# The seam between layer 0 and layer 2 of a four-layer graph kernel: layer 2's first slots over other rows, two tiles' lists gathered there, a weight split moved

## The chip, the cores and the metric

The kernel runs on one core of a Trainium2 chip. A core has engines that work in parallel, each in its own order: PE (TensorE, matrix products), DVE (VectorE) and ACT (ScalarE) for elementwise work, POOL (GpSimd), which here issues indirect transfers, and SP (SyncE), which issues the plain transfers. Sixteen DMA engines move the data between main memory and the on-chip buffers. The metric is the device time of one execution, in microseconds (us); lower is better. A time is the median of several runs.

## The reference

There are 2708 nodes with 512 features (fp32) and one matrix adj (2708 x 2708, nonnegative, mostly zero, denser towards low indices, its diagonal always set). Each of four layers normalizes x per row, applies a ReLU, computes something of it, and adds that to x:

```python
def layer(x, f):  return x + f(relu(layernorm(x)))
# layer 0
mask = (adj > 0); head = mask / sqrt(row_sum(mask))
inc = adj + head; f0 = (inc @ h) / row_sum(inc)
# layer 1: attention with 8 heads, scores - 1e16 * (1 - max(adj, eye)), softmax, values, Wo
# layer 2
h = relu(adj @ (h @ W1) + b1); h = relu(adj @ (h @ W3) + b3); f2 = tanh(h @ Wf + bf)
# layer 3
A = (adj != 0); f3 = A @ (h @ W + b) / column_sum(A)[:, None]
```

The mask of layer 1 is so large that each row's attention falls on the one column where max(adj, eye) is largest. Layer 1 is therefore a gather: with y = h (Wv Wo), row i adds y[argmax of row i].

## The kernel before, in words

Nodes are cut into 22 row tiles of 128 (the last has 20). A tile m's row of adj is used as a few dense 128x128 blocks (WHOLE[m], six at most) and as lists of 128 rows that hold a nonzero (CHUNKS[m], none for tile 0, 10 for tile 1, 9 for tile 2, then fewer). A list's rows of adj, transposed, and of the operand are fetched with indirect transfers on POOL. Tiles 0 to 2 (LEAD) use dense blocks for everything in layer 0, so their lists serve only layer 2 and later.

**Layer 0 and layer 1's y.** The loop over m forms a sum on PE (L866), the new x1 on DVE (L879), its normalization (L194 to L204), its transposes (L210), its product with Wv Wo (`yacc`, L176), the copy `yo` on ACT (L810) and the store of y on SP (L812). `after(m, ...)` holds the last four and runs one to two tiles behind. The stores wait in a list, `pending`, which `flush` issues at the next turn. The operands h of the sums are 128x512 rows (`h0`, `h6`, ...), which the gathers of `gather_rows` (L654) later reuse.

Each tile's whole row of adj (a slab `ar`, 1354 KB) must be scanned: `count_signs` on ACT with a Sign and a Relu pass, `attended` on DVE with a maximum with the identity (L622), MAX8 (L623) and FIND_INDEX8 (L624), which gives the column of the row's maximum. The tiles that are first in the program, 3 to 5 (FIRST) and 0 to 2 (ZERO), have their slabs loaded early for other ends and are scanned late: `LATE = FIRST + ZERO` are loaded again from turn m = 14 on, one a turn (`load_slab`), and scanned one turn later. After the loop, L914 copies the columns found to `idx`. `degrees` loads 18 pieces of counts (L386, SP), sums them on PE (L359) and ends in DVE operations (L368 to L380).

At m = 18 `gather_adj` gathers the lists of tiles 1 and 2 (19 indirect transfers, L635, POOL) and stores them to main memory (`listed`, L645, POOL). At m = 14 a weight W1 is loaded into `wr`, at m = 16 it is split into three parts hi, lo, s (`split_w`, `wa`; four ACT, eight DVE and four ACT operations, `split_b`, L215 to L225), and W3 is loaded into the same `wr`. Two operations named `behind` tie these to that turn.

**Layer 2.** For t = 0 to 21, `fetch(t)` loads x1 of the tile into a slot (L1170, SP) and gathers y by `idx` into another (L1172, POOL). Nine tiles are fetched ahead (AHEAD). Pool `g`, to which the slots belong, is the first one opened after layer 0; it lies where layer 0's slabs were. `first_product(t)` adds the two (L1184, DVE), stores x2 (L1185, SP), normalizes into the y slot, fetches tile t + 9, makes three parts of the ReLU of its transpose (`relu_parts`: transposes L983 on PE, `v_hi` L989 on ACT, `v_lo` and `v_s` on DVE), multiplies with W1's parts (`project3`, L1010, PE: `main` and `mixed`, or `agg` and `aggs` for odd t), drains the two into `go` (L968 on ACT, L969 on DVE) and stores it to `g1d` (L1193). `first_parts(t)` splits `go` into `ghi`, `glo`, `gs` for the dense products. `aggregated(m, ...)` forms adj's row tile times g1: raw blocks of adj (`raw`, L1029, SP) are marked as zero or not (`nz`, L1067, ACT), split (`a_hi` L1093, `a_lo` L1094) and multiplied (L1106); lists are loaded from `listed` (`load_listed`), marked too (`nz<-ac`, L1067) and multiplied with rows of g1 gathered from `g1d` (L1047, POOL). The gathers of g1 rows start when all 22 products are stored. Each finished tile is multiplied with W3 (`g2_rows`). W3 is split (`wb`) right after the nine fetches, and the biases b1, b3 (`load_bias`, L1156) are loaded before them.

The kernel is written in a layer that schedules: the order of instructions on each engine comes from a scheduler that takes the program's order and its own estimates. `tc.issue_after(instr)` makes what is inside follow `instr` in the order. [...]

Of the kernel before, what the change touches and what calls it, by code (L numbers as in the profile page):

```python
# [22 lines left out]
P = 128  # L23
# [21 lines left out]
def kernel(  # L45
# [41 lines left out]
    NCA = max(CHUNKS)  # L87
    NCL = max(CHUNKS[LEAD:])
# [66 lines left out]
    idx_g = const.tile([P, NT - 1, NCH], U32, name="idx_g")  # L155
# [79 lines left out]

    short = ctx.enter_context(ExitStack())
# [7 lines left out]
    with tc.tile_pool(name="l0_slab", bufs=2) as slabs, tc.tile_pool(  # L244
# [16 lines left out]
        idx_a = hp.tile([P, NT, NCH], U32, name="idx_a")  # L261
# [186 lines left out]
        def search(m):  # L448
# [9 lines left out]
            for c0 in range(0, CHUNKS[m], 8):  # L458
                c = slice(c0, c0 + 8)
                at = wp.tile([P, 8], U32, name="found")  # L460
                nc.vector.max_index(at, want[:, c], ranks)
                nc.vector.tensor_scalar(
                    index_g(m)[:, c],
                    at,
# [6 lines left out]
                    idx_a[:, m, c],  # L471
# [10 lines left out]
        def load_h0(ts):  # L482
            for t in ts:
                h0[t] = hp.tile([P, D], FP, name=f"h{t}")
                nc.sync.dma_start(out=h0[t][: rows(t)], in_=x[span(t)])
# [69 lines left out]
        LATE = FIRST + ZERO  # L555
# [72 lines left out]
        def gather_adj(m):  # L628

            n, num = rows(m), CHUNKS[m]  # L630
            for c0 in range(0, num, NCL):
                k = min(NCL, num - c0)
                ac = slabs.tile([P, NCL, P], FP, name="ac", bufs=3)
                for c in range(k):
                    nc.gpsimd.indirect_dma_start(  # L635
                        out=ac[:, c, :n],
                        out_offset=None,
                        in_=adj_units,
                        element_offset=dense_of(m) * P * N + m * P,
                        in_offset=bass.IndirectOffsetOnAxis(  # L640
                            ap=idx_a[:, m, c0 + c : c0 + c + 1], axis=0
                        ),
                    )
                if m < LEAD:
                    nc.gpsimd.dma_start(out=listed[m][:, c0 : c0 + k], in_=ac[:, :k, :n])  # L645
            gathers[m] = ac[:, :k, :n]

        def gather_rows(m):

            gs = []  # L650
            for c in range(CHUNKS[m]):
                g = hp.tile([P, D], FP, name=f"h{DENSE + gather_slot[0] % NGG}")
# [146 lines left out]
        def after(m, hn):  # L799
# [10 lines left out]
            nc.scalar.copy(yo[:n], yacc[:n])  # L810
# [18 lines left out]
        def flush():  # L829
            flush_counts()  # L830
            for issue in pending:
                issue()
            pending.clear()
# [20 lines left out]
        for m in range(NT):  # L854
# [48 lines left out]
            if m == NT - LEAD - 1:  # L903
                for t in range(1, LEAD):
                    gather_adj(t)
            if m == NT // 2 + 3:
                wr = load_w(wset, w1_d, "wr", lambda w: behind(w[:1, 0, :1], xt[:1, :1]))
            if m == NT // 2 + 5:
                w1 = split_w(
                    wset, wr, "wa", lambda w: behind(w[:1, :1], xt[:1, :1])  # L910
                )
                wr = load_w(wset, w3_d, "wr")
# [15 lines left out]

    gp = short.enter_context(tc.tile_pool(name="g", bufs=1))
# [96 lines left out]
    def load_piece(m, ts):  # L1026
        n, k = rows(m), rows(ts[0])
        raw = ap.tile([P, PIECE, P], FP, name="raw", bufs=3)
        nc.sync.dma_start(  # L1029
            out=raw[:k, : len(ts), :n],  # L1030
            in_=adj_t[ts[0] * P : ts[0] * P + k * len(ts), m * P : m * P + n].rearrange(
                "(t p) m -> p t m", p=k
            ),
        )
        return raw[:k, : len(ts), :n], k

    def load_listed(m):
        both = ap.tile([P, NCA + 1, P], FP, name="ac")
        ac = both[:, : CHUNKS[m], : rows(m)]
        nc.sync.dma_start(out=ac, in_=listed[m])  # L1040
# [16 lines left out]
    def aggregate(m, parts, shifted, gd, marked, bias):  # L1057
# [12 lines left out]
        chunks = []  # L1070
        if num:
            ac, spare = load_listed(m)
            if alone(m):
                nc.sync.dma_start(out=spare, in_=gd[span(m)])
                nc.vector.scalar_tensor_tensor(  # L1075
                    spare, spare, diag_c[:, m : m + 1], bias, op0=ALU.mult, op1=ALU.add
# [55 lines left out]
    def aggregated(m, parts, shifted, gd, bias, marked=False):  # L1132
        n = rows(m)
        u = wp.tile([P, D], FP, name="u")
        main, mixed, bias = aggregate(m, parts, shifted, gd, marked, bias)
# [817 lines left out]
```

## Time and profile before

| | us |
|---|---|
| median of 3 runs (1353.71 to 1357.23) | 1355.77 |
| the profiled execution, its own time | 1431.05 |
| span of the profiled execution, core 0 | 1429.2 |
| busy in that span: PE, DVE, ACT, POOL | 1218.8, 924.7, 693.2, 673.6 |
| last sum of layer 0 done | 488.0 |
| last store of y issued | 511.42 |
| first gather of y rows for layer 2 | 514.58 |
| first gather of g1 rows | 636.98 |

The last four rows are positions in the span of the profiled execution. In a timeline line of the profile, the first number is the start, the second the busy time, then engine, source line, operation and tiles; square brackets hold the idle time before it and what ended that. In a line of groups, the numbers after the bar are the total busy time, the mean of one in ns, and the idle time ahead. SPq is SP's queue of issues, PEld the loading of weights on PE.

### The profile page before, as it was taken

How to read it: one execution, taken by the hardware profiler on the slowest of the kernel's cores; microseconds unless marked ns; L12 is line 12 of the kernel's file. 1: busy time of each engine (PE TensorE's matmuls, PEld its weight loads, DVE VectorE, ACT ScalarE, POOL GpSimd, SP SyncE). 2: the span in 40 equal slices, each digit the busy share in tenths (PEclk: the TensorE clock that was granted, in tenths of full speed). 3: DMA queues.
4: the chain of work that ended last, by engine and by line, in shares of the span. 5: the costliest groups of instructions: out<-in, count | busy, mean ns of one | idle time of the engine just before them, and what ended most of it. 6: DMA issues, size and time to landing. Idle time of an engine off the chain costs nothing. (4 is left out here: it accounts for less than half of the span.)

```text
span 1429.2 us, 15148 instructions
## 1 busy us (share of the span) xinstructions
PE 1218.8 (85%) x4223; PEld 726.3 (51%) x4223; DVE 924.7 (65%) x1859; ACT 693.2 (49%) x1098; POOL 673.6 (47%) x703
## 2 busy tenths in 40 slices
PE   4985977769896848999989999899999999958797
PEld 2332433324343326765655655466666666646575
DVE  4664977768899857952343446356667685746576
ACT  5873563648635636642232224245555554634353
POOL 2245457555667441116645543245445344167663
PEclk9977998789988969999999999999999999979898
DMA  9976898778979477638888887856566666488785
GB/s 342 350 251 225 283 302 277 246 249 293 322 253 335 168 254 266 220 128 272 259 261 255 274 248 239 273 177 219 194 212 193 198 190 207 137 313 249 248 250 163
DMA packets 179342, 349.92 MB, mean 245 GB/s; under 512 B 22795, under 2 KB 85525, under 8 KB 175517
## 3 DMA queue, kind: packets, MB, share of 16 engines
q1 hardware_dynamic: 131648, 201.72, 41.5%
q0 software_dynamic: 46032, 145.05, 32.6%
q10 hardware_dynamic: 1568, 2.10, 0.4%
q8 instruction: 35, 0.57, 0.2%
q14 instruction: 59, 0.48, 0.1%
HBM read 285.97 MB, written 62.82 MB: 244 GB/s over the span
## 5 line engine op out<-in xcount | busy, mean ns | idle before, releaser
L1047 POOL DMA_INDIRECT gg<-g2d,idx_g x130 | 141.2, 1086 | 197.1 <-PE aggs L1110 149.3
L1110 PE MATMUL aggs<-gg,ac 128*128 128x512 f32 (+1 forms) x520 | 231.3, 593 | 3.2 <-DMA gg<-g1d,idx_g 2.1
L1047 POOL DMA_INDIRECT gg<-g1d,idx_g x130 | 130.7, 1005 | 159.1 <-PE aggs L1110 86.5
L635 POOL DMA_INDIRECT ac<-in_adj_t_dram,idx_a x130 | 132.7, 1021 | 91.9 <-issue 37.3
L866 PE MATMUL acc<-h,inc 128*128 128x512 f32 (+1 forms) x276 | 143.0, 664 | 37.4 <-DVE inc L706 29.2
L1110 PEld LDWEIGHTS aggs<-gg,ac 128*128 128x128 f32 (+1 forms) x520 | 97.0, 188 | 113.6 <-issue 102.2
L654 POOL DMA_INDIRECT h<-h0d,idx_g x111 | 114.8, 1034 | 83.7 <-PE acc L866 40.8
L866 PE MATMUL acc<-h,incl 128*128 128x512 f32 (+1 forms) x222 | 106.0, 620 | 0.8 <-issue 0.8
L866 PEld LDWEIGHTS acc<-h,inc 128*128 128x128 f32 (+1 forms) x276 | 54.9, 212 | 101.0 <-issue 60.2
L1075 DVE SCALAR_TENSOR_TENSOR ac<-ac,diag_c,bias 128x512 f32<-128x512 f32 x30 | 22.6, 754 | 100.8 <-DMA ac<-g1d 59.1
L1047 POOL DMA_INDIRECT gg<-hidr,idx_g x62 | 70.7, 1140 | 34.6 <-issue 20.8
L176 PE MATMUL yacc<-wvo,hT 128*128 128x512 f32 (+1 forms) x176 | 83.9, 615 | 1.7 <-ACT hT L211 1.0
L1106 PE MATMUL agg<-ghi,a_hi 128*128 128x512 f32 x180 | 77.3, 429 | 0.0
L1106 PE MATMUL agg<-glo,a_lo 128*128 128x512 f32 x180 | 73.4, 408 | 4.2 <-ACT glo L225 4.2
L1106 PE MATMUL aggs<-gs,a_s 128*128 128x512 f32 x180 | 73.1, 406 | 1.3 <-DVE gs L222 1.3
L990 DVE SCALAR_TENSOR_TENSOR v_lo<-pt,v_hi 128x512 fp32r<-128x512 f32 (+1 forms) x88 | 57.0, 658 | 16.2 <-ACT v_hi L989 13.9
L866 PEld LDWEIGHTS acc<-h,incl 128*128 128x128 f32 (+1 forms) x222 | 41.8, 195 | 50.0 <-issue 47.1
L623 DVE MAX8 tops<-ar 128x8 f32<-128x2708 f32 (+1 forms) x22 | 65.4, 2971 | 0.0
L624 DVE FIND_INDEX8 at_top<-tops,ar 128x8 uint32<-128x2708 f32 (+1 forms) x22 | 65.3, 2969 | 0.0
L989 ACT ACTIVATE v_hi<-pt 128x512 fp32r<-128x512 f32 (+1 forms) x88 | 48.2, 575 | 29.0 <-PE pt L983 22.1
L1139 DVE SCALAR_TENSOR_TENSOR u<-aggs,u 128x512 f32<-128x512 f32 x42 | 28.9, 687 | 50.9 <-PE aggs L1110 37.7
L1010 PE MATMUL main<-wb,v_hi 128*128 128x512 f32 (+1 forms) x176 | 56.7, 444 | 5.2 <-ACT v_hi L989 3.4
(355 smaller groups left out, 2777.9 us busy)
## 6 DMA issues: line engine op xcount, KB each, us to landing
ar<-in_adj_dram SPq DMA_DIRECT2D x27, 1354.0 KB
raw<-in_adj_t_dram SPq DMA_DIRECT2D x92, 192.0 KB
slot<-x SPq DMA_DIRECT2D x41, 256.0 KB
at<-in_adj_t_dram SPq DMA_DIRECT2D x26, 256.0 KB
h<-in_x_dram SPq DMA_DIRECT2D x21, 256.0 KB
h0d<-h POOLq DMA_DIRECT2D x21, 256.0 KB
xt<-in_x_dram SPq DMA_DIRECT2D x21, 256.0 KB
x<-xt SPq DMA_DIRECT2D x21, 256.0 KB
```

Of the source, the lines that this page charges most:

```text
L176: nc.tensor.matmul(acc[:n], hT[:, c, :n], w[:, c, :], start=(c == 0), stop=(c == NCD - 1))
L623: nc.vector.max(tops[:n, m, :], ar[:n])
L624: nc.vector.max_index(at_top[:n, m, :], tops[:n, m, :], ar[:n])
L635: nc.gpsimd.indirect_dma_start(out=ac[:, c, :n], out_offset=None, in_=adj_units, element_offset=dense_of(m) * P * N + m * P, in_offset=bas ...
L654: nc.gpsimd.indirect_dma_start(out=g, out_offset=None, in_=h0d[:, :], in_offset=bass.IndirectOffsetOnAxis(ap=index_g(m)[:, c : c + 1], axi ...
L866: product = nc.tensor.matmul(acc[:n], a, g, start=(i == 0), stop=(i == len(pairs) - 1))
L989: nc.scalar.activation(hi[d], pt[d], AF.Relu, scale=UP)
L990: nc.vector.scalar_tensor_tensor(lo[d], pt[d], 0.0, hi[d].bitcast(FP), op0=ALU.max, op1=ALU.subtract)
L1010: nc.tensor.matmul(acc[:n], a[:, c, :n], b[:, c, :], start=first and c == 0, stop=last and c == NCD - 1,)
L1047: nc.gpsimd.indirect_dma_start(out=gs[c], out_offset=None, in_=gd[:, :], in_offset=bass.IndirectOffsetOnAxis(ap=index_g(m)[:, c : c + 1], ...
L1106: turn(nc.tensor.matmul(acc[:n], a[:k, i, :n], b[:k], start=st, stop=sp))
L1110: nc.tensor.matmul(mixed[:n], a, g, start=(c == 0 and not dense_of(m)), stop=(c == len(chunks) - 1),)
```

## The change

1. Layer 0's h rows get a pool of their own (`l0_rows`), opened first, and layer 2's slots get one (`slots`), also opened first; so the slots lie where the h rows were.
2. `LATE` drops tile 0: tile 0 is scanned completely at the start, where its slab is loaded first, and one reload and one late scan go.
3. The lists of tiles 1 and 2 are gathered in layer 2, in `load_listed`, behind the ninth fetch, straight into the tile that is multiplied; two SP stores then write them to `listed`. Their indices are kept in `idx_lead`. In POOL's order these 19 gathers stand between fetches: nine fetches, three lists, fetch 9, seven lists, fetches 10 and 11, nine lists, fetch 12 and on.
4. W1 is split behind the last `yo`, and W3's load follows the last store of y. W3's split stands in `first_product(9)`; its first four ACT operations come out among the norms of the first products.
5. The biases b1 and b3 load behind the store of x2 of tile 2, the raw blocks behind the stores of x2 of tiles 0 and 1, the bias of layer 3 behind the last store of y.
6. `idx_g` is narrower (12 columns), `idx_a` holds tiles 3 and on only.

In the order of ACT's instructions, the marks `nz<-ac` of tiles 1 and 2 move: the first stands right behind the fourth tile's norm, the second twelve instructions further on, behind the fifth; before, they stood behind the sixth and the seventh.

The line numbers of the changed kernel are up to 24 higher from there on. The core of the diff:

```diff
...
@@ -152,7 +154,8 @@
-    idx_g = const.tile([P, NT - 1, NCH], U32, name="idx_g")
+    idx_g = const.tile([P, NT - 1, NCI], U32, name="idx_g")
+    idx_lead = const.tile([P, LEAD - 1, NCH], U32, name="idx_lead")
@@ -233,6 +236,7 @@
+    last_store, last_yo = [None], [None]
     short = ctx.enter_context(ExitStack())
@@ -241,7 +245,9 @@
-    with tc.tile_pool(name="l0_slab", bufs=2) as slabs, tc.tile_pool(
+    with tc.tile_pool(name="l0_rows", bufs=1) as hrows, tc.tile_pool(
+        name="l0_slab", bufs=2
+    ) as slabs, tc.tile_pool(
         name="l0_h", bufs=1
@@ -258,7 +264,7 @@
-        idx_a = hp.tile([P, NT, NCH], U32, name="idx_a")
+        idx_a = hp.tile([P, NT - LEAD, NCH], U32, name="idx_a")
@@ -459,16 +465,17 @@
                 nc.vector.max_index(at, want[:, c], ranks)
+                k = min(8, NCI - c0)
                 nc.vector.tensor_scalar(
-                    index_g(m)[:, c],
-                    at,
+                    index_g(m)[:, c0 : c0 + k],
+                    at[:, :k],
                     float(N - first),
...
                 nc.vector.tensor_scalar(
-                    idx_a[:, m, c],
+                    idx_a[:, m - LEAD, c] if m >= LEAD else idx_lead[:, m - 1, c],
                     at,
@@ -481,7 +488,7 @@
             for t in ts:
-                h0[t] = hp.tile([P, D], FP, name=f"h{t}")
+                h0[t] = hrows.tile([P, D], FP, name=f"h{t}")
                 nc.sync.dma_start(out=h0[t][: rows(t)], in_=x[span(t)])
@@ -552,7 +559,7 @@
         ZERO = list(range(LEAD))
-        LATE = FIRST + ZERO
+        LATE = FIRST + ZERO[1:]
         masks, row, slab = {}, {}, {}
@@ -628,28 +635,24 @@
             n, num = rows(m), CHUNKS[m]
-            for c0 in range(0, num, NCL):
-                k = min(NCL, num - c0)
-                ac = slabs.tile([P, NCL, P], FP, name="ac", bufs=3)
-                for c in range(k):
-                    nc.gpsimd.indirect_dma_start(
-                        out=ac[:, c, :n],
-                        out_offset=None,
-                        in_=adj_units,
-                        element_offset=dense_of(m) * P * N + m * P,
-                        in_offset=bass.IndirectOffsetOnAxis(
-                            ap=idx_a[:, m, c0 + c : c0 + c + 1], axis=0
-                        ),
-                    )
-                if m < LEAD:
-                    nc.gpsimd.dma_start(out=listed[m][:, c0 : c0 + k], in_=ac[:, :k, :n])
-            gathers[m] = ac[:, :k, :n]
+            ac = slabs.tile([P, NCL, P], FP, name="ac", bufs=3)
+            for c in range(num):
+                nc.gpsimd.indirect_dma_start(
+                    out=ac[:, c, :n],
+                    out_offset=None,
+                    in_=adj_units,
+                    element_offset=dense_of(m) * P * N + m * P,
+                    in_offset=bass.IndirectOffsetOnAxis(
+                        ap=idx_a[:, m - LEAD, c : c + 1], axis=0
+                    ),
+                )
+            gathers[m] = ac[:, :num, :n]
...
             for c in range(CHUNKS[m]):
-                g = hp.tile([P, D], FP, name=f"h{DENSE + gather_slot[0] % NGG}")
+                g = hrows.tile([P, D], FP, name=f"h{DENSE + gather_slot[0] % NGG}")
                 gather_slot[0] += 1
@@ -807,7 +810,7 @@
             yo = wp.tile([P, D], FP, name="yo")
-            nc.scalar.copy(yo[:n], yacc[:n])
+            last_yo[0] = nc.scalar.copy(yo[:n], yacc[:n]).ins
             pending.append(
@@ -829,7 +832,7 @@
             for issue in pending:
-                issue()
+                last_store[0] = issue().ins
             pending.clear()
@@ -900,16 +903,8 @@
                 score_bound(xt[:1, :1])
-            if m == NT - LEAD - 1:
-                for t in range(1, LEAD):
-                    gather_adj(t)
             if m == NT // 2 + 3:
                 wr = load_w(wset, w1_d, "wr", lambda w: behind(w[:1, 0, :1], xt[:1, :1]))
-            if m == NT // 2 + 5:
-                w1 = split_w(
-                    wset, wr, "wa", lambda w: behind(w[:1, :1], xt[:1, :1])
-                )
-                wr = load_w(wset, w3_d, "wr")
         flush()
@@ -926,6 +921,7 @@
+    slots = short.enter_context(tc.tile_pool(name="slots", bufs=1))
     gp = short.enter_context(tc.tile_pool(name="g", bufs=1))
@@ -1026,18 +1022,33 @@
         raw = ap.tile([P, PIECE, P], FP, name="raw", bufs=3)
-        nc.sync.dma_start(
-            out=raw[:k, : len(ts), :n],
-            in_=adj_t[ts[0] * P : ts[0] * P + k * len(ts), m * P : m * P + n].rearrange(
-                "(t p) m -> p t m", p=k
-            ),
-        )
+        with tc.issue_after(stored_x[0]):
+            nc.sync.dma_start(
+                out=raw[:k, : len(ts), :n],
+                in_=adj_t[ts[0] * P : ts[0] * P + k * len(ts), m * P : m * P + n].rearrange(
+                    "(t p) m -> p t m", p=k
+                ),
+            )
         return raw[:k, : len(ts), :n], k
-    def load_listed(m):
+    def load_listed(m, marked):
         both = ap.tile([P, NCA + 1, P], FP, name="ac")
         ac = both[:, : CHUNKS[m], : rows(m)]
-        nc.sync.dma_start(out=ac, in_=listed[m])
+        if marked and m < LEAD:
+            with tc.issue_after(last_fetch[0]):
+                for c in range(CHUNKS[m]):
+                    nc.gpsimd.indirect_dma_start(
+                        out=ac[:, c, :],
+                        out_offset=None,
+                        in_=adj_units,
+                        element_offset=dense_of(m) * P * N + m * P,
+                        in_offset=bass.IndirectOffsetOnAxis(
+                            ap=idx_lead[:, m - 1, c : c + 1], axis=0
+                        ),
+                    )
+            nc.sync.dma_start(out=listed[m], in_=ac)
+        else:
+            nc.sync.dma_start(out=ac, in_=listed[m])
         return ac, both[:, -NCD:, :].rearrange("p c k -> p (c k)")
@@ -1054,7 +1065,7 @@
-    def aggregate(m, parts, shifted, gd, marked, bias):
+    def aggregate(m, parts, shifted, gd, marked):
@@ -1067,13 +1078,13 @@
         mixed = ps_a.tile([P, D], FP, name="aggs")
-        chunks = []
+        chunks, bias = [], None
         if num:
-            ac, spare = load_listed(m)
+            ac, spare = load_listed(m, marked)
             if alone(m):
...
                 nc.vector.scalar_tensor_tensor(
-                    spare, spare, diag_c[:, m : m + 1], bias, op0=ALU.mult, op1=ALU.add
+                    spare, spare, diag_c[:, m : m + 1], biases[0 if marked else 1], op0=ALU.mult, op1=ALU.add
                 )
...
@@ -1156,36 +1168,47 @@
-    bias1 = load_bias(b1_d, "bias0")
-    bias3 = load_bias(b3_d, "bias1")
+    last_fetch, stored_x, biases = [None], [None], []
     xs, ys, g1, g1p = {}, {}, {}, {}
...
         n = rows(t)
-        xs[t] = gp.tile([P, D], FP, name=f"slot{t % AHEAD}")
+        xs[t] = slots.tile([P, D], FP, name=f"slot{t % AHEAD}")
         nc.sync.dma_start(out=xs[t][:n], in_=x1[t][:n])
-        ys[t] = gp.tile([P, D], FP, name=f"slot{AHEAD + t % AHEAD}")
-        nc.gpsimd.indirect_dma_start(
+        ys[t] = slots.tile([P, D], FP, name=f"slot{AHEAD + t % AHEAD}")
+        fetched = nc.gpsimd.indirect_dma_start(
             out=ys[t][:n],
...
         )
+        if t + 1 == AHEAD:
+            last_fetch[0] = fetched.ins
...
             return g1[t]
+        nonlocal wr
         n = rows(t)
...
         nc.vector.tensor_add(xt[:n], xt[:n], hn[:n])
-        nc.sync.dma_start(out=x2[t][:n], in_=xt[:n])
+        kept_x = nc.sync.dma_start(out=x2[t][:n], in_=xt[:n]).ins
+        if t < 2:
+            stored_x[0] = kept_x
+        if t == 2:
+            with tc.issue_after(kept_x):
+                biases.append(load_bias(b1_d, "bias0"))
+                biases.append(load_bias(b3_d, "bias1"))
         norm(wp, xt, n, hn)
...
             fetch(t + AHEAD)
+        if t == AHEAD:
+            w3.extend(split_w(wsetb, wr, "wb"))
+            wr = load_w(wset, wf_d, "wr")
         banks = (ps_a, ("agg", "aggs")) if t % 2 else ()
@@ -1203,8 +1226,11 @@
         fetch(t)
-    w3 = split_w(wsetb, wr, "wb")
-    wr = load_w(wset, wf_d, "wr")
+    with tc.issue_after(last_store[0]):
+        with tc.issue_after(last_yo[0]):
+            w1 = split_w(wset, wr, "wa")
+        wr = load_w(wset, w3_d, "wr")
+    w3 = []
@@ -1221,7 +1247,7 @@
             near = relu_parts(sums.pop(last), rows(last))
-        sums[m] = aggregated(m, first_parts, first_product, g1d, bias1, marked=True)
+        sums[m] = aggregated(m, first_parts, first_product, g1d, marked=True)
         if m == 0:
...
```

More of the change, by code (lines that the diff above doesn't have):

```diff
@@ L87 @@
     NCA = max(CHUNKS)
+    NCI = NCH - 4
+    assert all(num <= NCI for num in CHUNKS)
     NCL = max(CHUNKS[LEAD:])
@@ L1130, in aggregate, with aggregated @@
         return main, mixed, bias
-    def aggregated(m, parts, shifted, gd, bias, marked=False):
+    def aggregated(m, parts, shifted, gd, marked=False):
         n = rows(m)
         u = wp.tile([P, D], FP, name="u")
-        main, mixed, bias = aggregate(m, parts, shifted, gd, marked, bias)
+        main, mixed, bias = aggregate(m, parts, shifted, gd, marked)
+        bias = biases[0 if marked else 1] if bias is None else bias
         if dense_of(m):
@@ L1232 @@
     bf = load_bias(bf_d, "bias0")
-    bl = load_bias(b_d, "bias2")
+    with tc.issue_after(last_store[0]):
+        bl = load_bias(b_d, "bias2")
     g2, g2p, x3 = {}, {}, {}
@@ L1239, in second_product @@
             n = rows(t)
-            g2[t] = gp.tile([P, D], FP, name=f"slot{t % NSLOT}")
+            g2[t] = slots.tile([P, D], FP, name=f"slot{t % NSLOT}")
             nc.sync.dma_start(out=g2[t][:n], in_=g2d[span(t)])
@@ L1430, in x3_rows @@
             place = {order_2[-1]: "gs0", NSLOT: f"slot{order_2[-1]}"}.get(m, f"slot{m}")
-            xt = x3[m] = gp.tile([P, D], FP, name=place)
+            xt = x3[m] = (gp if place == "gs0" else slots).tile([P, D], FP, name=place)
         nc.sync.dma_start(out=xt[:n], in_=x2[m][:n])
@@ L1475 @@
             m = order_2[i]
-            sums[m] = aggregated(m, second_parts, second_product, g2d, bias3)
+            sums[m] = aggregated(m, second_parts, second_product, g2d)
             if m == 0:
```

## Prediction

> **What bounds the kernel now.** I read the page's slices first: PE is busy 85% of the span, and its digits dip near the middle, where layer 0 hands over to layer 2. The windows around that seam come next (columns: stretch, length, then busy us and instruction count of PE, PEld, DVE, ACT, POOL, then clock, DMA share, GB/s).
>
> ```profile
> 440.00:460.00 20.00, 12.13 (x25) 5.58 (x26) 20.00 (x36) 9.87 (x13) 16.65 (x12) 0.69 0.89 326
> 460.00:480.00 20.00, 19.76 (x55) 8.98 (x54) 20.00 (x31) 8.87 (x11) 6.87 (x9) 1.00 0.66 248
> 500.00:520.00 20.00, 9.76 (x43) 3.64 (x42) 7.54 (x21) 7.36 (x13) 9.50 (x11) 0.76 0.53 171
> 520.00:540.00 20.00, 12.15 (x44) 9.34 (x45) 15.45 (x39) 9.15 (x19) 8.64 (x9) 0.64 0.91 328
> 580.00:600.00 20.00, 19.75 (x86) 14.45 (x85) 19.10 (x51) 11.51 (x22) 2.80 (x3) 1.00 0.71 249
> ```
>
> Three regimes: DVE is full until 480 and PE waits for it once; from 500 to 540 nothing is full, so that stretch is a chain of latencies; from 580 PE is full. The timeline of that chain says what it consists of:
>
> ```profile
> 494.98 2.98 DVE L623 MAX8 tops<-ar 128x8 f32<-128x2708 f32 x1
> 497.88 0.20 DVE L201 TENSOR_SCALAR shift<-mv,rstd 128x1 f32<-128x1 f32 x1
> 511.42 0.31 SPq L812 DMA_DIRECT2D y<-yo  x1
> 514.58 1.34 POOL L1172 DMA_INDIRECT slot<-y,idx  x1 [6.11 <-ACT wb L225]
> 521.30 0.69 DVE L1184 TENSOR_TENSOR slot<-slot,slot 128x512 f32<-128x512 f32 x1 [4.31 <-DMA slot<-x]
> 526.91 1.09 PE L983 MATMUL pt<-ident,slot 128*128 128x128 f32 x4 [16.18 <-ACT slot L204]
> 528.04 0.60 ACT L989 ACTIVATE v_hi<-pt 128x512 fp32r<-128x512 f32 x1 [0.26 <-PE pt L983]
> ```
>
> The last y is stored at 511.42, its gather can start only then (514.58), the first sum x+y starts at 521.30, the first transposes at 526.91: PE waits 16.2 us. The sum waited last for x1's load, not for y. Upstream, the normalization of tile 20 (shift at 497.88) stood in DVE's order behind a late MAX8. Every first gather of layer 2's rows waits for the end of the products: 636.98 is my yardstick, since instruction order after about 600 us is the same in both kernels, and a shift there is carried to the end.
>
> **What the Trainium skill says.** "PSUM — Partial Sum Buffer", section "Engine vs sequencer instructions": "ScalarE/VectorE/GpSimdE queues are strict FIFO." The trace agrees: that 0.20 us shift sat behind a 2.98 us MAX8. "DMA: Bandwidth & Descriptors", section "Anatomy of one DMA — SWDGE (gpsimd) path", gives about 2.0 us plus bytes over 436 GB/s; for 256 KB that would be 2.6 us. The third y gather ended on POOL at 518.96 and its sum started at 524.50, 5.5 us later under load, so I use 2 to 4. The same page, "Issuing engines are not separate DMA queues", says transfers of all engines interleave; 520 to 540 with DMA at 0.91 fits. "TensorE: Matmul & The Clock Gate", section "What's actually happening": an idle window of about 3.4 us halves the clock. The first projection matmuls took 0.52 us (2.08 for four), later ones 0.27.
>
> **The parts.**
>
> 1. *One late pass less.* Tile 0 is scanned at the start: a second ACT pass (2.65 us) and MAX8, FIND_INDEX8 with a small one (6.2 us of DVE) go to the first 82 us, where DMA is near 1.0 and sum 0 waits for its slab. ACT's spare there was 5.4 us, DVE's nearly enough. Cost +1, from 0 to +4 if that cover is gone. At the end, five passes remain in place of six:
>
> ```profile
> L623 DVE MAX8 tops<-ar 128x8 f32<-128x2708 f32 x6 | 17.8, 2972 | 0.0
> L624 DVE FIND_INDEX8 at_top<-tops,ar 128x8 uint32<-128x2708 f32 x6 | 17.8, 2969 | 0.0
> L217 DVE TENSOR_TENSOR wa<-wr,wa 128x512 fp32r<-128x512 f32 x4 | 2.6, 672 | 0.0
> L222 DVE SCALAR_TENSOR_TENSOR wa<-wa,wa 128x512 fp32r<-128x512 f32 x4 | 2.6, 669 | 0.0
> ```
>
>    One pass is 2.97+2.97+0.29 = 6.2 us of DVE, and 5.3 us of ACT, and a 1354 KB load. The one at 494.98 stood directly before tile 20's shift.
>
> 2. *W1's split behind the last y.* It leaves 8x0.67 = 5.3 us of DVE and 4.7 of ACT in a stretch where DVE is full (440 to 480). With part 1 that is 11.5 us less DVE before the last y. PE had room: it waited 11.3 us for DVE's inc (L706). I replayed the order by hand: last y store at 499, not 511.42. **Gain 12** (6 if PE, 19.8 of 20 from 460, sets the pace and only the last pass counts; at most 14). The split itself then fills the hole that W3's filled before (511.3 to 517.5), at nothing; its cover is the flight of y.
>
> 3. *Slots over the h rows.* Nine x1 loads (SP) no longer wait for the slabs and are issued ahead of the last y stores; they cost those stores some 0.3 us each of SP's issue, which lies in the wait for yo. The first sum starts when y lands, 3.5 us after the gather, not 6.7. **Gain 3.** First v_hi at about 513 to 514 instead of 528.04. W3's load (1 MB) now starts when W1's split has read the buffer, near 504; W3's hi copies stand on ACT among the first norms and wait for it, 0 to 3 us.
>
> 4. *Lists of tiles 1 and 2.* 19 gathers at 0.94+0.30 us and four POOL stores (0.6 us and waits) leave POOL in 472 to 508. They were beside other work: gain 0. In layer 2, POOL issues nine fetches, three lists, fetch 9, seven lists, fetches 10 and 11, nine lists, fetch 12 and on. **This adds a wait.** On ACT the mark nz<-ac of tile 1 stands right behind the fourth norm, which I put at 522.5. With the first gather at 502, list 10 is issued by 502+20x1.25 = 527 and lands at 529 to 531. ACT stands 7.5 to 9 us; behind it are glo of tile 0, go (the drain) of product 1 and more norms, and through them PE and DVE. PE has three projections of some 4 us to do, so it loses less. The second mark comes at 538.5; 11 more issues bring tile 2's lists to 543 to 545: 5 to 6 us. Two SP stores of lists follow and nobody waits for them. Fetches 12 on are about 12 us later on POOL than their old place relative to fetch 8, but are read near T0+61. After both stalls, go of product 3, formerly 552.08, comes at 545 to 547: of 15 us, **6 are left**. What it replaces:
>
> ```profile
> 554.85 1.26 ACT L1067 ACTIVATE nz<-ac 128x1280 uint8<-128x1280 f32 x1
> 561.18 1.16 ACT L1067 ACTIVATE nz<-ac 128x1152 uint8<-128x1152 f32 x1 [2.01 <-DMA ac<-lst]
> ```
>
>    Those two, with the 2.0 wait, are 4.4 us of ACT that no longer lie further down: -2 to -3.
>
> 5. *W3's split at t = 9.* 5.3 us of DVE (8x0.67) and 4.7 of ACT land between 520 and 570, DVE being busy 15.2 to 16.4 of 20 there: +2, from 0 (it fits the gaps) to +5. A PE that idles once more runs some four matmuls at 0.52 instead of 0.27: +1.
>
> 6. *Biases, raw blocks behind x2 stores, narrower index tables.* Order on SP only; the first raw block is issued soon after the second sum and read after the first product: 0, from -1 (less competition) to +2 (a raw late at 545, where ACT already waited 3.0 for one). A trace of before cannot show the latter.
>
> Sum at the yardstick: -6 (state after the lists) -2.5 (marks) +2 (W3) +1 (clock) = -5.5. PE is full from 580 and starts that stretch earlier by the same amount, so it neither adds nor takes. With +1 from the start: -4.5, call it **-5**. Bounds: -14 with no list stall, +8 with the worst of the ends. The profiled execution took 1431.05 (span 1429.2), so about 1426 by its own clock; it lies 5.5% above the median of the runs, 1355.77. The shift consists mostly of fixed latencies and DVE work, so I carry it over unscaled: about 1351.
>
> **Rivals.**
>
> *A, slower: ACT's order behind POOL's list gathers.* Price: 20 POOL issues before tile 1's mark and 31 before tile 2's. For: the first two fetches were spaced 1.65 and 1.79 us, not 1.25, and DMA was at 0.91. At 1.65 each, tile 2's mark comes 12 us later than I reckon, near 556; the drains and norms behind it follow, PE gets some of it back. Net +5 to +7: about 1361. It decides from a spacing of about 1.45 us, or landing 6 us late. Against: the later seven fetches kept 1.25 to 1.5 at the same load.
>
> *B, larger gain.* The first three products' projections keep PE busy through ACT's wait, and PE, which is the bound from 580, starts its work 14 us earlier. For: PE's idle share of 520 to 560 is 12 us. Against: glo, go and v_hi are on ACT. Gain 11 to 15: about 1343.
>
> *C, no change.* PE sets the end of layer 0 (19.76 of 20), so part 2 brings 6, and the stalls take it: about 1355. For: PE is full in 460 to 480. Against: tile 20's shift waited for MAX8 itself. That the loads or the late pass don't move is hardly possible, since the order shows both.
>
> **Chances.** The likeliest 0.50 (-2 to -9, of it 0.38 beyond -0.3%, which is 4.1 us and about what a measurement of this kernel can tell from no change, 0.12 within), B 0.17, C 0.10 (within), A 0.23. So faster 0.55, same 0.22, slower 0.23. Range 1338 to 1363: B's and A's middles lie inside, their tails out. The likeliest case's own range is 1347 to 1354.
>
> **What would show it.** Right: MAX8 five times late; y store near 499, first y gather near 502, first transposes near 512; ACT's nz waiting for ac's gathers twice, 8 and 5 us; wb's split around product 9; first g1d gather near 631. Wrong: y store after 505 (part 2), nz waits summing to over 15 us (A) or under 5 (B), a start longer by over 4 us (part 1), or a wait of PE on W3.

## The result, and the profile after

The changed kernel takes 1369.25 us (median of 5 runs, 1365.44 to 1371.87) against 1355.77 for the kernel before (5 runs, 1351.97 to 1357.23): ratio 1.0103, 95% interval 1.0076 to 1.0130. It is slower by 13.5 us where 4.8 less were forecast, and lies outside the range of 1338 to 1363.

Executions of one and the same kernel took either about 1355 or about 1435 us, and the profile of before shown above (1431.05) is of the longer kind, the profile after (span 1364.0) of the shorter, so the kernel before was profiled once more (span 1352.7, called "before, again") to set like beside like.

Timeline of the changed kernel: last y store, first y gather, first sum, first transposes, the marks of the lists, SP's stores of the lists, first gather of g1 rows.

```profile
462.06 0.30 SPq L815 DMA_DIRECT2D y<-yo  x1
464.60 1.31 POOL L1183 DMA_INDIRECT slot<-y,idx  x1 [47.95 <-DVE wa L225]
468.34 0.69 DVE L1198 TENSOR_TENSOR slot<-slot,slot 128x512 f32<-128x512 f32 x1 [0.80 <-DMA slot<-y,idx]
472.68 0.70 DVE L1198 TENSOR_TENSOR slot<-slot,slot 128x512 f32<-128x512 f32 x1 [2.92 <-DMA slot<-y,idx]
473.30 0.17 DVE L199 BATCH_NORM_AGGREGATE mv<-stats 128x2 f32<-128x6 f32 x1
477.28 1.12 PE L979 MATMUL pt<-ident,slot 128*128 128x128 f32 x4 [15.91 <-ACT slot L207]
493.70 0.34 SPq L1049 DMA_DIRECT2D lst<-ac  x1
493.75 1.27 ACT L1078 ACTIVATE nz<-ac 128x1280 uint8<-128x1280 f32 x1 [5.03 <-DMA ac<-in_adj_t_dram,idx_lead]
507.64 1.16 ACT L1078 ACTIVATE nz<-ac 128x1152 uint8<-128x1152 f32 x1 [5.56 <-DMA ac<-in_adj_t_dram,idx_lead]
507.68 0.32 SPq L1049 DMA_DIRECT2D lst<-ac  x1
597.63 0.97 POOL L1058 DMA_INDIRECT gg<-g1d,idx_g  x1 [43.74 <-DMA nz<-nz]
```

The same anchors in the timeline of before, again:

```profile
457.91 0.31 SPq L812 DMA_DIRECT2D y<-yo  x1
461.23 1.19 POOL L1172 DMA_INDIRECT slot<-y,idx  x1 [5.38 <-ACT wb L225]
467.84 0.69 DVE L1184 TENSOR_TENSOR slot<-slot,slot 128x512 f32<-128x512 f32 x1 [4.36 <-DMA slot<-x]
582.75 1.39 POOL L1047 DMA_INDIRECT gg<-g1d,idx_g  x1 [44.26 <-DMA nz<-nz]
```

Two losses show. The last y store is 4.2 us **later** (462.1 against 457.9), not 12 earlier. And the stretch from the first y gather to the first g1 gather, called **the seam** from here on, is 133.0 us long, not 121.5 as in before, again, nor 129 as forecast (from 502 to 631). Both marks wait for POOL's gathers, as forecast; SP's stores of the lists end their wait at the same moments.

Windows of the changed kernel over the seam, in the columns explained above:

```profile
460.00:480.00 20.00, 3.24 (x10) 1.50 (x9) 12.25 (x30) 9.01 (x18) 12.05 (x12) 0.63 0.69 229
480.00:500.00 20.00, 13.56 (x56) 10.34 (x54) 12.00 (x26) 11.14 (x22) 15.13 (x17) 0.84 0.94 305
500.00:520.00 20.00, 15.16 (x54) 11.05 (x54) 12.69 (x26) 9.78 (x18) 6.88 (x7) 0.85 0.62 191
560.00:580.00 20.00, 19.75 (x85) 13.77 (x84) 13.29 (x34) 10.18 (x20) 0.00 (x0) 1.00 0.26 92
```

No engine is full from 480 to 520. PE fills up only at 560 (from 520 to 540 it has 17.8 of 20 us, from 540 to 560 18.4; DVE has 19.5 in the first of these). The groups from 370 to 455 us confirm that one late scan is gone (five in place of six; FIND_INDEX8 likewise):

```profile
L630 DVE MAX8 tops<-ar 128x8 f32<-128x2708 f32 x5 | 14.8, 2967 | 0.0
```

From these two traces (sum k is the DVE operation that makes x1 of the loop's tile k), the difference of 11.3 us in the spans splits up so:

| stretch | before, again | changed | difference |
|---|---|---|---|
| start to sum 0 | 82.4 | 83.1 | +0.8 |
| sum 0 to sum 1 | 22.6 | 18.8 | -3.9 |
| sum 1 to sum 13 | 213.2 | 228.8 | +15.6 |
| sum 13 to last y store | 139.7 | 131.3 | -8.3 |
| last y store to first y gather | 3.3 | 2.5 | -0.8 |
| the seam | 121.5 | 133.0 | +11.5 |
| first g1 gather to the end | 770.0 | 766.4 | -3.6 |

The second and the third row belong together: from sum 0 to sum 13 the changed kernel takes 11.7 us longer. Nearly all of that shows in two places, where PE, DVE and ACT stand still together, for 7.3 us from 232.9 and for 3.1 from 289.2. This is the first of them, a window and what ends it:

```profile
233.00:240.00 7.00, 0.00 (x0) 0.00 (x0) 0.00 (x0) 0.00 (x0) 5.22 (x6) 0.75 0.79 247
240.23 0.15 DVE L461 CAST ends<-ranks 128x1 f32<-128x1 f16 x1 [7.52 <-DMA ranks<-rank_b]
240.57 0.29 ACT L201 ACTIVATE rstd<-mv,eps 128x1 f32<-128x1 f32 x1 [7.68 <-DVE mv L199]
240.93 0.16 PE L606 MATMUL list<-ones_b,sgn 128*128 128x1 bf16 x1 [8.04 <-ACT rstd L201]
```

DVE waits for the load of `ranks`, and ACT and PE for what stands behind that in DVE's order. In before, again the three engines have no common halt of 1.5 us in this stretch; the same two operations on DVE wait 1.9 and 3.2 us there for `ranks`, but another engine works through it.

### The profile page after: what moved, and what is told of

It is laid out like the page before. It is cut to its first block, busy times and chain, and to the rows that moved or that the text cites. A ratio compares the mean times of both kernels' runs of the same rounds, so it can differ in the third digit from the quotient of the medians.

```text
span 1364.0 us, 15120 instructions
## 1 busy us (share of the span) xinstructions
PE 1208.5 (89%) x4223; PEld 722.8 (53%) x4223; DVE 924.3 (68%) x1853; ACT 688.9 (51%) x1095; POOL 671.9 (49%) x699
## 4 chain that ended last, share of the span: by engine, by line
PE 42%; DMA 10%; DVE 4%; issue 2%; ACT 2%; POOL 2%; SPq 0%; DVEq 0%; ACTq 0%; POOLq 0%
PE aggs L1121 13%; PE main L1006 8%; PE agg L1117 5%; PE mixed L1006 4%; PE aggs L1117 3%; PE pt L979 2%; DMA gg<-hidr,idx_g 2%; DMA ac<-g1d 1%; PE aggs L1135 1%; PE aggs L1347 1%; PE agg L1006 1%; DMA raw<-in_adj_t_dram 1%; DMA wa<-hidr,idx_g 1%; POOL gg L1058 1%; PE agg L1347 1%
## 5 line engine op out<-in xcount | busy, mean ns | idle before, releaser
L869 PE MATMUL acc<-h,inc 128*128 128x512 f32 (+1 forms) x276 | 144.3, 664 | 18.5 <-DVE inc L709 12.7
L640 POOL DMA_INDIRECT ac<-in_adj_t_dram,idx_a x111 | 114.6, 1033 | 48.2 <-issue 27.4
L869 PE MATMUL acc<-h,incl 128*128 128x512 f32 (+1 forms) x222 | 100.4, 600 | 0.0
L1086 DVE SCALAR_TENSOR_TENSOR ac<-ac,diag_c,bias 128x512 f32<-128x512 f32 x30 | 22.6, 753 | 86.3 <-DMA ac<-g1d 58.7
L1183 POOL DMA_INDIRECT slot<-y,idx x22 | 23.0, 1044 | 89.9 <-DVE wa L225 47.9
```

Source lines behind the costliest of these rows:

```text
L640: nc.gpsimd.indirect_dma_start(out=ac[:, c, :n], out_offset=None, in_=adj_units, element_offset=dense_of(m) * P * N + m * P, in_offset=bas ...
L869: product = nc.tensor.matmul(acc[:n], a, g, start=(i == 0), stop=(i == len(pairs) - 1))
```

## The experiments

Theories. **Lists**: the seam is longer because in-order queues stand behind POOL's list gathers. **Split**: W3's split among the products costs more than W1's did. **Start**: scanning tile 0 early costs more than it saves, by its own work or (**order**) because the scheduler then puts out another order for layer 0. The table gives what each profile shows. There is one profile for each kernel, and a position can be off by some us: the one of undo_lists is the fastest of its 20 runs (1346.41, their median is 1360.58), that of late_marks the slowest of its five (1372.13, median 1365.00).

| kernel | sums 0 to 13 | sums 1 to 13 | last y store | seam | ratio to before (95%) |
|---|---|---|---|---|---|
| before, again | 235.9 | 213.2 | 457.9 | 121.5 | |
| changed | 247.6 | 228.8 | 462.1 | 133.0 | 1.0103 (1.0076 to 1.0130) |
| undo_lists | 241.7 | 222.9 | 454.8 | 123.5 | 1.0056 (1.0032 to 1.0079) |
| undo_split | 250.9 | 230.4 | 468.4 | 131.6 | 1.0119 (1.0057 to 1.0181) |
| undo_late | 234.9 | 211.1 | 452.7 | 135.6 | 1.0078 (1.0049 to 1.0107) |
| late_marks | 250.3 | 228.3 | 469.2 | 127.8 | 1.0104 (1.0061 to 1.0146) |
| only_late | 247.6 | 228.3 | 467.2 | 122.8 | 1.0136 (1.0069 to 1.0202) |
| undo_lists_late | 233.5 | 209.3 | 452.2 | 122.8 | 0.9985 (0.9958 to 1.0011) |
| late_marks_undo_late | 237.6 | 215.0 | 451.2 | 129.5 | 1.0043 (1.0019 to 1.0066) |
| held_d | 249.9 | 230.9 | 460.3 | 134.0 | 1.0077 (1.0052 to 1.0102) |
| late_marks_stores_d | 234.1 | 208.4 | 457.6 | 120.8 | 0.9970 (0.9944 to 0.9996) |

**before_again**, the kernel before without an edit.

> The kernel before, unchanged, for a profile whose layer 0 is not stretched. All theories expect the same time as the kernel before; wanted are the positions of the last y store, the first y gather and the first g1 gather, against 462.1, 464.6 and 597.6 in the changed kernel. If the change loses only in the seam (theory: lists), the last y store lies 8 to 14 us later than in the changed kernel, and the stretch from the first y gather to the first g1 gather is 122 us, not 133. If the start or layer 0 lost time (theory: start), the last y store is no later than in the changed kernel.

Measured: one time, 1354.46. The last y store is earlier than in the changed kernel, so layer 0 lost too, not the seam alone.

**undo_lists**: lists gathered at turn 18 of layer 0 again.

```diff
...
+            if m == NT - LEAD - 1:
+                for t in range(1, LEAD):
+                    gather_adj(t)
...
-        if marked and m < LEAD:
+        if False:
```

> The changed kernel with the lists of tiles 1 and 2 gathered in layer 0 again, at turn 18, and loaded by SP in layer 2. Theory lists (ACT's marks stand behind POOL's gathers): the two waits of 5.0 and 5.6 us go, the stretch from first y gather to first g1 gather falls from 133 to about 123, and the kernel takes 1357 to 1361. Theory start or split: 1367 to 1370, the stretch stays over 130.

The seam falls to 123.5: the lists are its loss. In time 0.5% comes back, not all.

**undo_split**: W1 split at turn 16, W3 with the first fetches.

```diff
+            if m == NT // 2 + 5:
+                w1 = split_w(
+                    wset, wr, "wa", lambda w: behind(w[:1, :1], xt[:1, :1])
+                )
+                wr = load_w(wset, w3_d, "wr")
...
-    with tc.issue_after(last_store[0]):
-        with tc.issue_after(last_yo[0]):
-            w1 = split_w(wset, wr, "wa")
-        wr = load_w(wset, w3_d, "wr")
-    w3 = []
+    w3 = split_w(wsetb, wr, "wb")
+    wr = load_w(wset, wf_d, "wr")
```

> The changed kernel with W1 split at turn 16 of layer 0 and W3 split with the first fetches, as before. Theory split (W3's 8 DVE and 8 ACT operations in the middle of the products cost more than what W1's cost in layer 0): 1360 to 1364. Theory lists: the last y store 4 to 6 us later, the stretch of products 2 to 3 us shorter, 1369 to 1373.

Last y store 6.4 later, seam 1.5 shorter, time (four runs) not distinguishable from the changed kernel's: nothing speaks for theory split. From sum 13 to the last y store it takes 135.1 us against 131.3: W1's move is worth 3.8 there.

**undo_late** and **only_late**: the same line, changed back in the changed kernel (as shown) and changed alone in the kernel before (the other way round).

```diff
-        LATE = FIRST + ZERO
+        LATE = FIRST + ZERO[1:]
```

> The changed kernel with tile 0 scanned late again (six late passes, none at the start). Theory start (the pass at the start costs more than the late one did): 1359 to 1364. Theory lists: the start is 1 us shorter, the last y store 6 to 8 us later, 1374 to 1378.

> The kernel before with one edit: tile 0 is scanned at the start, not late. Theory order (with the early scan the scheduler puts out another order for layer 0's middle, in which DVE and PE wait for one another): sum 2 is ready at 142 to 150 as in the changed kernel (146.4), not at 134 to 139; the last y store comes at 458 to 466 in spite of one late pass less; slower by 2 to 9 us. Rival (my prediction's sum: +1 at the start, -6 to -8 at the end): last y store at 450 to 453, faster by 5 to 7 us.

undo_late's last y store is 9.4 us *earlier* with one late scan *more*; its seam keeps the loss. only_late is slower, by 1.36% as a ratio, by 0.9% going by the medians (1364.94 of four runs, one of them 1377.81, against 1353.13); sum 2 comes at 148.2 and the last y store at 467.2. So the early scan costs, alone and in company. In company the ratio of undo_late alone would not show it, since its interval overlaps that of the changed kernel; undo_lists and undo_lists_late below, which differ in this line only, have intervals apart. In all six kernels of the table that scan tile 0 early, sums 0 to 13 take 242 to 251 us (sums 1 to 13 223 to 231); in the five that scan it late, 233 to 238 (208 to 215). PE, DVE and ACT halt together for at least 1.5 us at a time in five of the six (all but held_d), for 6 to 10 us in sum, and in none of the five. Windows from sum 1 to sum 13 of before, again:

```profile
105.00:318.24 213.24, 199.41 (x635) 90.51 (x635) 192.61 (x372) 138.05 (x196) 150.97 (x151) 0.97 0.95 329
```

and of only_late:

```profile
103.79:332.04 228.25, 203.24 (x633) 93.24 (x634) 194.65 (x377) 139.76 (x196) 154.44 (x156) 0.94 0.92 318
```

DVE has nearly the same work, 193 and 195 us, but idles 34 us in place of 21. What it waited for there, in before, again (waits on DVE: total, times, longest):

```profile
DVE inc L698 <- DMA at<-in_adj_t_dram: 7.5, 4, 4.5
DVE ends L455 <- DMA ranks<-rank_b: 5.1, 2, 3.2
...
DVE diag_c L600 <- PE list L599: 0.3, 1, 0.3
```

and in only_late:

```profile
DVE ends L455 <- DMA ranks<-rank_b: 12.2, 4, 4.7
DVE diag_c L600 <- PE list L599: 7.9, 3, 5.7
DVE inc L698 <- DMA at<-in_adj_t_dram: 4.8, 3, 2.6
```

The waits for `ranks`, which layer 0 stores and loads again, and for `list`, a small product whose place in PE's order is behind a sum's products (in the changed kernel ten matmuls, 8.1 us, stood ahead of one), grew from 5.4 to 20.1 us, more than the whole difference in idle time; the wait for the load of `at` fell by 2.7. Why the early scan makes these waits longer is not settled by that.

**late_marks**: only the two marks moved, behind the drain of product 12.

```diff
...
-            if marked:
+            if marked and m < LEAD:
+                with tc.issue_after(late_go[0]):
+                    mark(whole, ac)
+            elif marked:
                 mark(whole, ac)
```

> The changed kernel with only the two marks of the lists (nz<-ac of tiles 1 and 2, ACT) moved behind the drain of product 12; the lists are still gathered by POOL between the fetches. Theory ACT order (the marks hold up ACT's queue while POOL gathers): the waits of 5.0 and 5.6 us go, the stretch from the first y gather to the first g1 gather falls from 133 to 123-126, the time by 7 to 10 us. Rival (POOL's 19 gathers delay fetches 9 to 12, or their 1.2 MB crowd the DMA engines): the stretch stays at 130 or more.

Neither side is right: the seam falls to 127.8, half of the loss, and the time does not fall with it (1.0104 where the changed kernel has 1.0103). ACT's longest wait is now another one, and SP's timeline names what is behind it. The waits of ACT from 500 to 600 us:

```profile
ACT go L964 <- DMA g1d<-go: 10.4, 1, 10.4
```

SP's timeline of the same kernel:

```profile
504.16 0.49 SPq L1027 DMA_DIRECT2D raw<-in_adj_t_dram  x1
515.68 0.32 SPq L1050 DMA_DIRECT2D lst<-ac  x1
516.10 0.38 SPq L1223 DMA_DIRECT2D g1d<-go  x1
```

SP issues nothing from 504.7 to 515.7: it waits, in order, for the second tile's lists to store them. Behind it stands the store of a `go`, and a later drain (520.84) needs that buffer.

**undo_lists_late** and **late_marks_undo_late** put the edits above together.

> The changed kernel with lists gathered in layer 0 and tile 0 scanned late, both as before; the slots over the h rows, the moved weight splits, biases and raw blocks stay. If lists (10 us in the seam) and tile 0 (9 us in layer 0) are independent costs of what is left over: last y store at 450 to 455, stretch 121 to 125, and 2 to 8 us faster than the kernel before. If the rest of the change costs something too: equal to the kernel before or slower.

> The changed kernel with the marks behind product 12 and tile 0 scanned late. Theory ACT order plus theory order: last y store at 450 to 455, stretch 122 to 126, 2 to 10 us faster than the kernel before. If POOL's gathers in the seam cost by themselves: stretch over 130 and no faster than the kernel before.

With both losses undone, the rest of the change (slots, splits, biases, raw blocks) cannot be told from the kernel before: 0.9985, and the interval holds 1. The two items together make the whole loss. The last y store comes 5.7 us earlier than in before, again. With the marks moved and the lists still in layer 2, the seam stays at 129.5, with 8.4 us in one wait of the drain for g1's store.

**late_marks_stores**: that kernel, with SP's stores of the lists behind the store of product 12 as well.

```diff
...
-            nc.sync.dma_start(out=listed[m], in_=ac)
+            with tc.issue_after(late_g1[0]):
+                nc.sync.dma_start(out=listed[m], in_=ac)
```

**held**: the changed kernel, tile 0 early, each later scan held behind the loop's last x1 in DVE's order.

```diff
...
-                else:
+                elif last_xt[0] is not None:
+                    with tc.issue_after(last_xt[0]):
+                        attended(t)
+                else:
                     attended(t)
```

after_b is the changed kernel again, and held_marks_stores has the edits of held together with the moved marks and stores; endings _b to _d mark repetitions.

> The changed kernel with tile 0 scanned late, the two marks behind product 12 (ACT) and the two stores of the lists behind g1's store of product 12 (SP). Theory SP order (in the run with late marks alone, SP's stores of the lists stood ahead of g1's stores, a drain waited 10.4 us for its buffer, and the stretch stayed at 129.5): this wait goes and the stretch from first y gather to first g1 gather falls to 121-125, last y store at 450 to 453, 2 to 8 us faster than the kernel before. Rival (POOL's 19 gathers between the fetches, or the crowd on the DMA engines): the stretch stays at 128 or more.

> The changed kernel, tile 0 scanned at the start as there, but each later scan (MAX8 and FIND_INDEX8) held behind the x1 of the loop's last finished turn in DVE's order; in DVE's order only two scans then stand between sums 1 and 2, not three. Theory order (what is lost in layer 0 is lost to another order of instructions, not to the start's own work): sum 2 at 132 to 140 as with the late scan, last y store earlier than the changed kernel's 462.1 by 3 to 10 us. Rival (the early scan costs by itself, through DVE time or slab buffers at the start): sum 2 and the last y store as in the changed kernel, within 2 us.

> The same kernel as late_marks_stores (tile 0 scanned late, marks behind product 12, the lists' stores behind g1's store of product 12), once more, since that pair of runs fell in a time in which the kernel before took 1437 us. Theory SP order: stretch from first y gather to first g1 gather 121 to 125, 2 to 8 us faster than the kernel before. Rival (POOL's gathers between the fetches or the crowd on the DMA engines): stretch 128 or more.

> The same kernel as held (tile 0 scanned at the start, later scans held behind the loop's last x1), once more. Theory order: sum 2 at 132 to 140, last y store at 452 to 459. Rival (the early scan costs by itself): sum 2 near 146 and last y store at 460 to 464, as in the changed kernel.

> The changed kernel again, beside the others of this call on the same chip: slower than the kernel before by 1.0 to 1.3%; sum 2 at 146 to 150, last y store at 460 to 469, stretch 131 to 135.

> The changed kernel with later scans held behind the loop's last x1, marks behind product 12, lists' stores behind g1's store of product 12: tile 0 stays scanned at the start. If both theories of order hold (layer 0's and the queues' in the seam): last y store at 448 to 458, stretch 121 to 125, as fast as late_marks_stores_b or faster. If the early scan costs by itself: 8 to 12 us slower than late_marks_stores_b.

> The same kernel as late_marks_stores (tile 0 scanned late, marks and the lists' stores behind product 12), meant for a time in which the kernel before takes about 1355 us. Theory SP order: stretch from first y gather to first g1 gather 121 to 125, 2 to 8 us faster than the kernel before. Rival (POOL's gathers between the fetches or the crowd on the DMA engines): stretch 128 or more.

> The same kernel as held_marks_stores (tile 0 scanned at the start, later scans held behind the loop's last x1, marks and stores behind product 12), for such a time. Theory order in layer 0: sum 2 at 132 to 142, last y store at 448 to 458, no slower than late_marks_stores_c. If the early scan costs by itself: last y store at 460 or later, 8 to 12 us slower than late_marks_stores_c.

> The same kernel as held (the changed kernel with later scans held behind the loop's last x1), for a time in which the kernel before takes about 1355 us. Theory order in layer 0: sum 2 at 132 to 142, last y store at 452 to 459, 3 to 9 us faster than the changed kernel. Rival (the early scan costs by itself): sum 2 near 146, last y store at 460 to 469, as the changed kernel.

> The same kernel as late_marks_stores, for such a time. Theory SP order: stretch from first y gather to first g1 gather 121 to 125. Rival (POOL's gathers or the crowd on the DMA engines): 128 or more.

In the first eight of these ten the kernel before took 1430 to 1437 us. Their ratios to it: late_marks_stores 1.0030 (0.9998 to 1.0063), _b 1.0105 (1.0045 to 1.0164), _c 1.0074 (1.0043 to 1.0105); held 1.0009 (0.9980 to 1.0038), held_b 1.0038 (1.0007 to 1.0068); held_marks_stores 1.0042 (1.0009 to 1.0075), _c 1.0038 (1.0008 to 1.0069); the changed kernel 1.0103 (1.0027 to 1.0179). The positions expected of them were missed by all: where the last y store was put at 448 to 469, it came at 508 to 528. Their seams ran from 132 to 139 us whatever was moved. So they decide nothing between the theories, and they are no support for theory SP order: the one profile of before that took as long has a seam of 122.4.

In the last two the kernel before took 1354.19. Timeline of late_marks_stores_d:

```profile
460.12 1.31 POOL L1190 DMA_INDIRECT slot<-y,idx  x1 [55.23 <-DVE wa L225]
580.92 1.41 POOL L1060 DMA_INDIRECT gg<-g1d,idx_g  x1 [47.35 <-issue]
```

The seam is 120.8, as expected by theory SP order, and no drain waits for g1's store any more: from 129.5, moving the stores as well was worth 8.7. Here POOL's 19 gathers between the fetches cost nothing once no queue stands behind them; for the runs at 1430 us and more, with their seams of 132 to 137 for the same kernel, that is not shown. The ratio, 0.9970, is the only one of the table whose interval lies below 1, and it does so barely (to 0.9996); the same kernel at 1430 us and more was not faster than before.

held_d: sum 2 at 140.4 as expected, two scans ahead of it in DVE's order, not three, but the last y store (460.3) misses the expected 452 to 459, and sums 1 to 13 still take 230.9 us, with DVE waits of 11.8 for `ranks` and 6.7 for `list`. That length is not quite comparable: fourteen scans lie in it where the changed kernel has thirteen, so it holds 6 us more of DVE's work and the stretch from sum 13 to the last y store less (125.6 against 131.3). DVE's idle time in it fell from 34.2 to 28.0, and the common halts are gone. All in all holding the scans won 1.8 us at the last y store. That the early scan costs is shown; that the *order* it leads to is the cause, rather than something else it brings, is argued from these waits and stays open.

## Why the prediction was wrong

The prediction's own marks show where it went wrong. It had the last y store 12 us earlier; it came 4.2 later, a miss of some 16 us. It had the seam at 129, 6.6 us longer than the 122.4 of its profile; it became 11.5 longer, a miss of 5.

- **Part 1, one late pass less.** This is the step that failed most. "Cost +1, from 0 to +4" priced the first 82 us, and there it was right (+0.8 to sum 0). The middle of layer 0 was put at nothing, without a reason, and the price lay there: 11.7 us from sum 0 to sum 13 (+15.6 from sum 1 on, -3.9 before it), of which 10.4 are the two common halts. How 6 us of work at the start bring about waits some 200 and 260 us later is open; another order of instructions is the likely link. The gain at the end, 12 with part 2, measured 8.3.
- **Part 2, W1's split.** Right in kind: 3.8 us of those 8.3, estimated at about half of 12.
- **Part 3, the x1 loads.** The first sum did start 3.7 us after the gather, not 6.6. The gain of 3 was 0: the aggregation of tile 0's statistics (473.30) stands in DVE's order behind the second sum, which waits 2.92 us for the second y. The first transposes come 12.7 us after the first gather, before 12.2. I named the wait that ended last for one instruction, and not what was late next.
- **Part 4, the lists.** ACT's waits were there at 29.1 and 43.0 us after the first gather, against 27 to 29 and 41 to 43 forecast, and were rather shorter (5.0 and 5.6 us against 7.5 to 9 and 5 to 6). What was too small is what they and their surroundings cost: a net 6.5 us (9 of the 15 gained, less 2.5 for the old marks), where gathering the lists in layer 0 again gave back 9.5 (133.0 to 123.5), or 12.8 beside undo_late (135.6 to 122.8). PE, which was to lose less than ACT's waits (10.6 us), stood idle for 11.2 of the 40 us from 480 to 520. One sentence was also wrong: "Two SP stores of lists follow and nobody waits for them." With the marks out of the way the stores hold up SP, g1's stores behind them, the drains' two buffers, and PE: 8.7 us. In the changed kernel itself this cost is hidden: no drain waits for g1's store there, because ACT stands at its marks for the same gathers. Moving the marks alone shortened the seam by 5.2 us (133.0 to 127.8), or 6.1 beside undo_late. The stores were never moved without the marks, so how the loss divides between the two queues is open.
- **Part 5, W3's split**, and **part 6** were small, as forecast: without part 4 the whole rest leaves the seam at 122.8 to 123.5, against 121.5.
- **Rival A** named the right side and the wrong quantity: the 31 issues up to tile 2's last list took 1.31 us each on average and landed on time, so its point of decision was not reached; the loss came at the forecast landing times. (It also misread one spacing: the last two of the nine fetches before lay 1.72 us apart, not 1.25 to 1.5.) **Rival B**: PE did not keep busy through the waits (13.6 and 15.2 of 20 us from 480 to 520). **Rival C** expected 6 us at the end of layer 0, all taken by the stalls; 8.3 were won there, and more than that was lost before.
- Starting from a profile at 1431 us misled neither the seam (122.4 there, 121.5 in before, again) nor the end of layer 0: in before, again the two windows of 20 us in the same place, 386.5 to 426.5, have DVE at 20.00 too and PE at 13.1 and 19.4. What it stretched ahead of the seam is sum 0 to sum 13 (288.3 against 235.9), the part that the forecast left out.

## What to carry to other kernels

An instruction that waits for something late holds up its whole queue, and a store that nobody reads is no exception (here SP stood 11 us at one): list, for each queue with a new wait (SP's issues too), what stands behind it and whose buffer that frees. Late results were best marked and stored behind work that is later still. And where a scheduler decides the order, work moved from one place to another can have its price anywhere in between: compare the stretches between fixed points of the program, not the ends alone, and look for moments in which all engines stand still.

## What the runs showed of the hardware

The issue of indirect gathers on POOL hardly slowed down under load: in the changed kernel, from 480 to 500 with the DMA engines busy at 0.94, most came 1.25 us apart (0.95 busy and 0.30 idle) and the slowest 1.62. What grew was the time from issue to use: 3.7 us for the first y gather, with the DMA engines busy at 0.43 on average in that time, and 6.5 for the second (issued at 466.22, used at 472.68), with 0.85.
